# A four-level perceiver block on one Trainium2 core: first tile asked for first, the first MLP's norms interleaved between tiles, time mixing with its weights on ScalarE

## The chip, the cores and the metric

The kernel runs on one core of a Trainium2 chip. The metric is device time in microseconds (us) of one execution; three runs of the kernel before are given. One further execution was recorded by the hardware profiler. Engines are named as in the profile: PE is TensorE (PEld its weight loads), DVE is VectorE, ACT is ScalarE, POOL is GpSimd, SP is SyncE, which issues most transfers.

## The reference, cut to what matters

The input x has 8 sequences of 64 rows with 256 channels, 512 rows in all, in fp32; a context of 8 x 1601 x 128 stands beside it. Twelve blocks follow each other, each x = x + block(layernorm(x)): four levels of cross-attention over the context, self-attention or time mixing, and a mixture of experts. Two of them are touched. The first is level 0's cross-attention, which is a self-attention with an MLP, and then an attention over the context with an MLP:

```python
def _mha(x, y, ...):                                  # layernorm with gain and bias: _ln
    o = attention(_ln(x, lnx_g, lnx_b), _ln(y, lny_g, lny_b))
    x_out = x + o @ li1_w + li1_b
    h = gelu(_ln(x_out, ln3_g, ln3_b) @ li2_w + li2_b)
    return x_out + h @ li3_w + li3_b

x = _ln(xx, ln1_g, ln1_b)
x = x + _mha(x, x, a1...)          # self-attention, mask of future keys behind the softmax
x = _ln(x, ln2_g, ln2_b)
return x + _mha(x, ee, a2...)      # over the context
```

The second is level 1's time mixing, over k, v and r, three products of x mixed with its predecessor in the sequence:

```python
def step(carry, kv):               # one step in time, per channel
    aa, bb, pp = carry
    ww = u + kt;  p = maximum(pp, ww)
    y = (exp(pp - p) * aa + exp(ww - p) * vt) / (exp(pp - p) * bb + exp(ww - p))
    p2 = maximum(pp + w, kt);  e1b = exp(pp + w - p2);  e2b = exp(kt - p2)
    return (e1b * aa + e2b * vt, e1b * bb + e2b, p2), y
out = (sigmoid(r) * y) @ Wo        # w = -exp(time_decay), u = time_first
```

## The kernel before, in words

The 512 rows lie as NI = 4 tiles of P = 128 rows, `X[:, i, :]`, on the chip for the whole kernel. The outer order is the order of the blocks; inside a block the loops run over the four tiles, over the 16 heads and, for attention over the context, over 8 batches and 13 tiles of 128 context rows (KT). All transfers of weights, rows and the context are asked for on SP's queue, in program order, into rotating pools. Within an engine's queue, instructions run in order; what order they are put in is chosen by a scheduler from the program's text and dependencies, except where `manual_schedule(engines=...)` or `keep_in_program_order` fixes it. `FLASH` (L621) names PE, ACT and DVE for such regions.

A norm is `norm_of` (L343 to L347: statistics `bn_stats`, `bn_aggr`, eps added on DVE, then power -0.5 on GpSimd, 128x1) and `norm_by` (L351, subtract the mean and multiply, on DVE). `normed_tile` is both in one. Each norm so goes from DVE to GpSimd and back.

The start (L283 to L325, L1318 to L1326): x, `const` (identity, masks, rope tables), `cols` (per-channel gains and biases) and four weights are asked for, then three rows that are spread over all partitions: ln1_g, ln1_b, a1li1_b. `begin(i)` norms tile i, norms it again, multiplies by ln1_g, adds ln1_b, norms it a third time for the attention, and lets GpSimd make `xo` = x + a1li1_b. The transposes pst (L438), scaled on DVE (L446), feed the products psq and psk (L455), then the scores psS (L505).

The first MLP (L1395 to L1417): `norm1` and `enter1` run staggered over the tiles, with two base sums per tile on GpSimd (L1401, L1402); `turn_into` (L1279) transposes a tile on PE and scales its first chunk on ACT (L1289), its second on DVE (L1287). `after_attention` (L1299) is li2 with Gelu (psl, L396; L1303), then `meanwhile()`, then li3 (psn, L405), which calls `leave1(i)` for each tile: add base, norm, times ln2_g, plus ln2_b, norm again, and `turn2(i-2)`. Here `meanwhile` is `context_norm` (L1370): 12 GpSimd operations make `shift` for a later rope, statistics of the first context batch on DVE (L1355), four operations of `scales` on GpSimd (L1360 to L1363), 13 normalisings on ACT (L1368). Then follows a2wq (psl, 16 products) and the attention over the context.

The block m2 (L1489 to L1513) comes behind that attention: GpSimd makes x1r = x1 + a2li1_b and base = X + x1 + a2li3_b, four tiles each; the product of li1 gives psn, and `attended(i)` adds x1r, norms, and turns tile i-2 by `enter2`; GpSimd adds `xo` to base. Then the second MLP, whose last addition writes X.

Time mixing (L1677 to L1744) works channel-major: `xT` has 2 chunks (NC_) of 128 channels by 512 rows. Three mixings on DVE (L1694, L1695), three products on PE; kk and vv are copied out of PSUM, rr is a sigmoid on ACT (L1700). Per chunk: a scan for the running maximum pp (L1720), five differences on DVE with four exponentials on ACT for e1, e2, f1, f2 (L1721 to L1730), two scans for bb and aa (L1733, L1734), numerator and denominator, reciprocal (L1740), the product with rr, yy (L1743), and Wo (psn, L405).

## Time and profile before

| what | value |
|---|---|
| runs | 2094.94, 2100.58, 2097.62 us; median 2097.62 |
| profiled execution | 2095.15 us; its span 2093.4, 1.75 around it |
| granted PE clock, mean over the span | 0.947 |
| PE busy | 1885.6 us (90%) |
| DVE, ACT, POOL busy | 1246.5, 1031.0, 310.1 us |

The timeline gives start, duration, engine, line and operation, with out<-in by tile names; x16 means sixteen instructions in a row that were folded into one line, and the bracket holds the engine's idle time before it and what ended it. In the table of stretches, a busy time is followed by the number of instructions; PEclk is the clock that PE was granted, as a share of full speed. The places that the diff touches lie at 0 to 30 us (start), 83 to 133 us (first MLP), 585 to 605 us (m2) and 858 to 905 us (time mixing).

### The profile page before, as it was taken

Reading aid. Unit: us, or ns where it says so; the run is one execution under the profiler, and the core shown is the slowest. Engines: PE = TensorE matmul, PEld = TensorE weight load, DVE = VectorE, ACT = ScalarE, POOL = GpSimd, SP = SyncE. Lnnn points to the kernel's source line nnn. Section 1 sums busy time; section 2 is a strip of 40 time slices with the busy share of each in tenths; the row PEclk is TensorE's granted clock in tenths of the full one; section 3 lists DMA queues with packets and bytes.
Section 4 is the critical chain, followed back from the end, with each engine's and each line's share of the span. In section 5 each row is a group of like instructions: output and inputs, shape, how many; then the busy total and the mean of one; then the engine's idle time right before and its main releaser. Section 6 shows DMA issues by size and latency. Waiting matters only on the chain. (4 is left out here: it accounts for less than half of the span.)

```text
span 2093.4 us, 35785 instructions
## 1 busy us (share of the span) xinstructions
PE 1885.6 (90%) x14818; PEld 1363.0 (65%) x14818; DVE 1246.5 (60%) x2118; ACT 1031.0 (49%) x1703; POOL 310.1 (15%) x391
## 2 busy tenths in 40 slices
PE   5878999999989898659999999999967899998889
PEld 4545777777758475338757777778834566666747
DVE  5546666666716423660266666665634588888743
ACT  2326777777612222301166565654212788888323
POOL 3301111111033221030000000000023011211124
PEclk9989999999989898859999999999979999999989
DMA  8310000000005207215500010000422101000313
GB/s 299 113 56 1 18 17 17 18 17 11 1 30 213 86 28 268 103 43 197 181 17 33 33 33 33 33 17 16 177 78 82 39 18 34 18 18 16 137 56 112
DMA packets 37939, 142.16 MB, mean 68 GB/s; under 512 B 4904, under 2 KB 17712, under 8 KB 32208
## 3 DMA queue, kind: packets, MB, share of 16 engines
q1 hardware_dynamic: 32448, 128.18, 17.2%
q0 software_dynamic: 3696, 10.11, 1.4%
q8 instruction: 118, 1.93, 0.4%
q10 hardware_dynamic: 1632, 1.57, 0.2%
q14 instruction: 45, 0.37, 0.1%
HBM read 129.21 MB, written 19.71 MB: 71 GB/s over the span
## 5 line engine op out<-in xcount | busy, mean ns | idle before, releaser
L866 PEld LDWEIGHTS psav<-cn,raw 128*128 128x128 f32 (+1 forms) x3328 | 402.3, 191 | 87.1 <-issue 85.8
L801 DVE TENSOR_TENSOR raw<-raw,mb 128x1024 f32<-128x1024 f32 (+1 forms) x336 | 383.9, 1146 | 61.3 <-ACT mb L797 61.3
L866 PE MATMUL psav<-cn,raw 128*128 128x129 f32 (+1 forms) x3328 | 406.7, 275 | 0.7 <-ACT raw L805 0.7
L854 PE MATMUL psS<-qk,ct 128*128 128x512 f32 (+1 forms) x832 | 397.2, 599 | 7.5 <-ACT raw L855 7.5
L780 DVE TENSOR_TENSOR top<-raw,top 128x1024 f32<-128x1024 f32 (+1 forms) x240 | 271.4, 1131 | 143.1 <-ACT raw L855 121.8
L805 ACT ACTIVATE raw<-raw 128x1024 f32<-128x1024 f32 (+1 forms) x336 | 335.8, 1002 | 15.8 <-DVE raw L801 14.4
L855 ACT COPY raw<-psS 128x512 f32<-128x512 f32 (+1 forms) x416 | 236.6, 588 | 126.4 <-PE psS L854 123.2
L854 PEld LDWEIGHTS psS<-qk,ct 128*128 128x128 f32 (+1 forms) x832 | 138.1, 187 | 115.0 <-issue 81.5
L976 ACT COPY raw<-psS 128x1024 f32<-128x1024 f32 (+1 forms) x112 | 105.3, 940 | 2.0 <-PE psS L971 1.7
L774 DVE TENSOR_TENSOR top<-raw 128x1024 f32<-128x1024 f32 x48 | 58.8, 1225 | 71.1 <-ACT raw L855 37.7
L971 PEld LDWEIGHTS psS<-qz,kT 32*128 32x128 f32 (+1 forms) x1664 | 54.8, 181 | 61.2 <-ACT raw L976 42.2
L1215 PE MATMUL psgd<-w,xdT 128*128 x272 | 92.5, 472 | 1.5 <-DVE xdT L1204 1.5
L347 POOL TENSOR_TENSOR mv<-mv,mhalf 128x1 f32<-128x1 f32 x76 | 42.4, 562 | 339.5 <-DVE mv L346 319.0
L971 PE MATMUL psS<-qz,kT 32*128 32x128 f32 (+1 forms) x1664 | 76.9, 295 | 15.2 <-ACT raw L976 14.9
L992 PE MATMUL psav<-raw,v 128*32 128x128 f32 (+1 forms) x1664 | 86.3, 279 | 3.6 <-ACT raw L805 3.5
L992 PE MATMUL psav<-raw,ones 128*32 128x128 f32 (+1 forms) x1664 | 83.6, 273 | 0.0
L469 POOL MEMSET vz<- 128x528 f32 (+1 forms) x12 | 7.5, 644 | 427.6 <-PE pso L1853 427.4
L1241 POOL DMA_INDIRECT answered<-rows,homes x53 | 51.0, 963 | 95.7 <-ACT rows L1239 53.0
L1215 PEld LDWEIGHTS psgd<-w,xdT 128*128 128x128 f32 x272 | 48.6, 194 | 21.2 <-issue 9.0
L797 ACT COPY mb<-psmb 128x512 f32<-128x512 f32 x48 | 28.2, 588 | 67.3 <-PE psmb L795 67.1
L949 PE MATMUL psk<-ct,w_x3kv_None 128*128 128x401 f32 (+1 forms) x128 | 58.0, 539 | 0.7 <-issue 0.7
L959 PE MATMUL psv<-w_x3kv_None,ct 128*128 128x256 f32 (+1 forms) x208 | 55.6, 387 | 0.0
(429 smaller groups left out, 2829.4 us busy)
## 6 DMA issues: line engine op xcount, KB each, us to landing
cn<-in_cn_dram SPq DMA_DIRECT2D x24, 838.5 KB, 4.5
ct<-in_ct_dram SPq DMA_DIRECT2D x24, 800.5 KB, 4.5
dealt<-in_deal_dram SPq DMA_DIRECT2D x3, 2955.5 KB, 25.9
w<-in_f0w_dram SPq DMA_DIRECT2D x8, 1088.0 KB, 15.8
w_f1up<-in_f1up_dram SPq DMA_DIRECT2D x8, 1024.0 KB, 4.8
w_f1dn<-in_f1dn_dram SPq DMA_DIRECT2D x8, 1024.0 KB, 4.8
w<-in_f2w_dram SPq DMA_DIRECT2D x8, 1024.0 KB, 14.1
w<-in_f3w_dram SPq DMA_DIRECT2D x16, 384.0 KB, 7.8
```

The costliest lines, as they stand in the source:

```text
L774: nc.vector.tensor_tensor(hd["top"], hd["raw", 0], raw, ALU.max)
L780: nc.vector.tensor_tensor(top[:n, :m, :], raw, top[:n, :m, :], ALU.max)
L801: nc.vector.tensor_tensor(raw, raw, halves[h]["mb"][:n].unsqueeze(1).to_broadcast([n, m, 512]), ALU.add)
L805: nc.scalar.activation(raw, raw, AF.Exp)
L854: nc.tensor.matmul(x[:n], ct[:, kt * P : kt * P + n], qk, start=True, stop=True)
L855: nc.scalar.copy(raw[:n, i, :], x[:n])
L866: nc.tensor.matmul(oa[:, j // 2, j % 2 * CO : (j % 2 + 1) * CO], w[:n, i, j * P : (j + 1) * P], cn[:n, kt, :], start=kt == 0 and j % 2 == ...
L949: nc.tensor.matmul(t[:, : hi - lo], wkv[:, c * P : (c + 1) * P], cts[b][:, lo:hi], start=True, stop=True)
L971: nc.tensor.matmul(x[:n, g, i * P : (i + 1) * P], kTs[h][r, kt * P : kt * P + n], qzs[b][r, c].rearrange("p m s -> p (m s)"), start=True, ...
L976: nc.scalar.copy(raw[:n, :m, :].rearrange("p i (g s) -> p i g s", g=4), x[:n, :, : m * P].rearrange("p g (i s) -> p i g s", s=P))
L992: nc.tensor.matmul(oa[r, at * P : (at + 1) * P], what, w[:n, i, g * P : (g + 1) * P], start=kt == 0 and at == 0, stop=kt == KT - 1 and at ...
L1215: nc.tensor.matmul(y[:, :m], st[t]["xT"][:, k, :], w[:, bass.ds(x + at + k * m, m)], start=k == 0, stop=k == C // P - 1)
```

## The change

1. Start. Tile 0 of x is asked for alone and first; the rows ln1_g and ln1_b are asked for right behind it, on ACT's queue; `const` comes in two parts, the rope tables after the first weights, the rest of x after `cols`. In `begin`, the second norm's scaling and the two row operations become two `scalar_tensor_tensor`.
2. `turn_into` scales both chunks on ACT.
3. `context_norm` writes the two scaled tables to one temporary of two parts, and keeps its statistics in program order.
4. `leave1` uses the same two combined operations, and `norm_by` of tile i-1 (`scale2`) stands between the statistics and the use of tile i's; the MLP from li2 to the last `turn2` lies in a region of fixed order on PE, ACT, DVE and POOL (`FOUR`).
5. The sums xo = x1 + a2li1_b, X += x1, X += a2li3_b (12 on GpSimd) stand right behind the first MLP; m2 keeps X += xo only, with `norm_by` one tile late, and the second MLP adds straight into X.
6. Time mixing: k and r stay in PSUM; v is copied on ACT; the scaling in the mixing of v and r is on ACT; the pairs e1, e2 and f1, f2 are exp(-relu(d)) and exp(-relu(-d)) of one difference d, on ACT; sigmoid becomes a factor 1 + min(exp(-r), 1e36) in the denominator.

```diff
@@ -281,11 +281,16 @@
 X = keep.tile([P, NI, C], F32, tag="X", name="X")
-nc.sync.dma_start(X.rearrange("p i c -> p (i c)"), d["x"])
+nc.sync.dma_start(X[:, 0, :], d["x"][:, :C])
+first_rows = [rpool.tile([P, C], F32, tag="r", name="row") for _ in range(2)]
+for k, t in zip(("ln1_g", "ln1_b"), first_rows):
+    nc.scalar.dma_start(t, d["rows"][row_at[k] : row_at[k] + 1, :].partition_broadcast(P))
 const = keep.tile([P, d["const"].shape[1]], F32, tag="const", name="const")
-nc.sync.dma_start(const, d["const"])
+n0 = const_at["r0c"][0]
+nc.sync.dma_start(const[:, :n0], d["const"][:, :n0])
 cols = keep.tile([P, d["cols"].shape[1]], F32, tag="cols", name="cols")
 nc.sync.dma_start(cols, d["cols"])
+nc.sync.dma_start(X[:, 1:, :].rearrange("p i c -> p (i c)"), d["x"][:, C:])
@@ -619,6 +624,7 @@
+FOUR = FLASH | {mybir.EngineType.Pool}
@@ -1282,11 +1288,9 @@
     for c in range(C // P):
-        d = dst[:, c, i * P : (i + 1) * P]
-        if c:
-            nc.vector.tensor_scalar(d, t[:, c * P : (c + 1) * P], col(pair[0], c), col(pair[1], c), ALU.mult, ALU.add)
-        else:
-            nc.scalar.activation(d, t[:, c * P : (c + 1) * P], AF.Identity, bias=col(pair[1], c), scale=col(pair[0], c))
+        nc.scalar.activation(
+            dst[:, c, i * P : (i + 1) * P], t[:, c * P : (c + 1) * P], AF.Identity, bias=col(pair[1], c), scale=col(pair[0], c)
+        )
@@ -1310,7 +1314,8 @@
     li1 = chunks(weight("a1li1"), C)
-    g1, b1, r1 = row("ln1_g"), row("ln1_b"), row("a1li1_b")
+    nc.sync.dma_start(const[:, n0:], d["const"][:, n0:])
+    (g1, b1), r1 = first_rows, row("a1li1_b")
@@ -1318,9 +1323,9 @@
             normed_tile(y, X[:, i, :])
-            normed_tile(x, y)
-            nc.vector.tensor_tensor(x, x, g1, ALU.mult)
-            nc.vector.tensor_tensor(x, x, b1, ALU.add)
+            mv = norm_of(y)
+            nc.vector.scalar_tensor_tensor(x, y, mv[:, 0:1], g1, ALU.subtract, ALU.mult)
+            nc.vector.scalar_tensor_tensor(x, x, mv[:, 2:3], b1, ALU.mult, ALU.add)
@@ -1352,7 +1357,7 @@
-            nc.vector.bn_stats(st, cns[b][:, kt, :CY])
+            tc.keep_in_program_order(nc.vector.bn_stats(st, cns[b][:, kt, :CY]))
             nc.vector.bn_aggr(mvs[b][:, kt, 0:2], st)
@@ -1372,10 +1377,10 @@
                 cs, sn = (K(x)[:, c * P : (c + 1) * P] for x in ("r0c", "r0s"))
-                tmp = mp.tile([P, P], F32, tag="turned", name="turned", bufs=2)
-                nc.gpsimd.tensor_scalar(tmp, sn, col(k + "s", c), None, ALU.mult)
-                nc.gpsimd.tensor_scalar(dst, cs, col(k, c), None, ALU.mult)
-                nc.gpsimd.tensor_tensor(dst, dst, tmp, ALU.add)
+                tmp = mp.tile([P, 2, P], F32, tag="turned", name="turned", bufs=2)
+                nc.gpsimd.tensor_scalar(tmp[:, 0], sn, col(k + "s", c), None, ALU.mult)
+                nc.gpsimd.tensor_scalar(tmp[:, 1], cs, col(k, c), None, ALU.mult)
+                nc.gpsimd.tensor_tensor(dst, tmp[:, 0], tmp[:, 1], ALU.add)
 @@ -1389,8 +1394,8 @@
-        xn, z = (nat.tile([P, NI, C], F32, tag="nat", name="xn") for _ in range(2))
-        mvs1 = {}
+        xn = nat.tile([P, NI, C], F32, tag="nat", name="xn")
+        mvs1, mvs2 = {}, {}
@@ -1401,23 +1406,36 @@
         def leave1(i, t):
...
             nc.vector.tensor_tensor(x, t, base[:, i, :], ALU.add)
-            normed_tile(z[:, i, :], x)
-            nc.vector.tensor_tensor(x, z[:, i, :], g2, ALU.mult)
-            nc.vector.tensor_tensor(x, x, b2, ALU.add)
-            normed_tile(xn[:, i, :], x)
+            mv = norm_of(x)
+            scale2(i - 1)
+            nc.vector.scalar_tensor_tensor(x, x, mv[:, 0:1], g2, ALU.subtract, ALU.mult)
+            nc.vector.scalar_tensor_tensor(x, x, mv[:, 2:3], b2, ALU.mult, ALU.add)
+            mvs2[i] = norm_of(x)
             turn2(i - 2)
...
+        def scale2(i):
+            if i >= 0:
+                norm_by(xn[:, i, :], x1[:, i, :], mvs2[i])
...
         staggered(norm1, enter1)
-        after_attention("a1", xo, x3, mp, ps, leave1, context_norm)
-        turn2(NI - 2)
-        turn2(NI - 1)
+        with tc.manual_schedule(engines=FOUR):
+            after_attention("a1", xo, x3, mp, ps, leave1, context_norm)
+            turn2(NI - 2)
+            scale2(NI - 1)
+            turn2(NI - 1)
...
+        r1, r3 = row("a2li1_b"), row("a2li3_b")
+        for i in range(NI):
+            for dst, one, two in ((xo, x1[:, i, :], r1), (X, X[:, i, :], x1[:, i, :]), (X, X[:, i, :], r3)):
+                tc.keep_in_program_order(nc.gpsimd.tensor_tensor(dst[:, i, :], one, two, ALU.add))
     for dealt in dealts:
@@ -1487,31 +1505,30 @@
         with general() as ps, tc.tile_pool(name="m2", bufs=1) as mp:
-            r1, r3 = row("a2li1_b"), row("a2li3_b")
-            base, x1r = (mp.tile([P, NI, C], F32, tag=k, name=k) for k in ("base", "x1r"))
                 xn = nat.tile([P, NI, C], F32, tag="nat", name="xn")
-            for i in range(NI):
-                nc.gpsimd.tensor_tensor(x1r[:, i, :], x1[:, i, :], r1, ALU.add)
-            for i in range(NI):
-                nc.gpsimd.tensor_tensor(base[:, i, :], X[:, i, :], x1[:, i, :], ALU.add)
-                nc.gpsimd.tensor_tensor(base[:, i, :], base[:, i, :], r3, ALU.add)
+            mvs2 = {}
...
+            def scale2(i):
+                norm_by(xn[:, i, :], xo[:, i, :], mvs2[i])
+                nc.gpsimd.tensor_tensor(X[:, i, :], X[:, i, :], xo[:, i, :], ALU.add)
...
             def enter2(i):
                 turn_into(ps, x3, i, xn[:, i, :], ("a2ln3_g", "a2ln3_b"))
-                nc.gpsimd.tensor_tensor(base[:, i, :], base[:, i, :], xo[:, i, :], ALU.add)
...
             def attended(i, t):
-                nc.vector.tensor_tensor(xo[:, i, :], t, x1r[:, i, :], ALU.add)
-                normed_tile(xn[:, i, :], xo[:, i, :])
+                nc.vector.tensor_tensor(xo[:, i, :], t, xo[:, i, :], ALU.add)
+                mvs2[i] = norm_of(xo[:, i, :])
+                if i > 0:
+                    scale2(i - 1)
                 if i > 1:
...
             enter2(NI - 2)
+            scale2(NI - 1)
             enter2(NI - 1)
-            after_attention(
-                "a2", xo, x3, mp, ps, lambda i, t: nc.vector.tensor_tensor(X[:, i, :], t, base[:, i, :], ALU.add), lambda: None
-            )
+            after_attention("a2", xo, x3, mp, ps, into_X, lambda: None)
@@ -1687,61 +1704,75 @@
-    kk, vv, rr = big("kk"), big("vv"), big("rr")
-    for n, (k, w, dst) in enumerate((("k", wkv[:, 0:2], kk), ("v", wkv[:, 2:4], vv), ("r", wro[:, 0:2], rr))):
-        mixed = pool.tile([P, NC_, NT], F32, tag="mixed", name="mixed", bufs=2)
-        for c in range(NC_):
-            nc.vector.tensor_scalar(mixed[:, c, :], xT[:, c, :], col("time_mix_" + k, c), None, ALU.mult)
-            nc.vector.scalar_tensor_tensor(
-                b4(mixed)[:, c, :, 1:], b4(xT)[:, c, :, : S - 1], om[:, 2 * n + c : 2 * n + c + 1],
-                b4(mixed)[:, c, :, 1:], ALU.mult, ALU.add,
-            )
-        if k == "r":
-            lin_T(ps, w, mixed, C, lambda c, t: nc.scalar.activation(rr[:, c, :], t, AF.Sigmoid))
-        else:
-            lin_T(ps, w, mixed, C, lambda c, t: evac(dst[:, c, :], t))
...
+    at = lambda x, c: b4(x)[:, c]
+    old, new = (lambda x, c: at(x, c)[:, :, : S - 1]), (lambda x, c: at(x, c)[:, :, 1:])
+    first = lambda x, c: at(x, c)[:, :, 0:1]
+    head = lambda t: t.rearrange("p (b s) -> p b s", s=S)[:, :, 1:]
...
+    vv = big("vv")
+    kk, pr = {}, {}
+    leaves = (
+        lambda c, t: kk.update({c: t}), lambda c, t: nc.scalar.copy(vv[:, c, :], t), lambda c, t: pr.update({c: t}),
+    )
+    for n, (k, w) in enumerate((("k", wkv[:, 0:2]), ("v", wkv[:, 2:4]), ("r", wro[:, 0:2]))):
+        mixed = pool.tile([P, NC_, NT], F32, tag="mixed", name="mixed", bufs=2)
+        for c in range(NC_):
+            share = col("time_mix_" + k, c)
+            if n:
+                nc.scalar.activation(mixed[:, c, :], xT[:, c, :], AF.Copy, scale=share)
+            else:
+                nc.vector.tensor_scalar(mixed[:, c, :], xT[:, c, :], share, None, ALU.mult)
+            nc.vector.scalar_tensor_tensor(
+                new(mixed, c), old(xT, c), om[:, 2 * n + c : 2 * n + c + 1], new(mixed, c), ALU.mult, ALU.add,
+            )
+        lin_T(ps, w, mixed, C, leaves[n])
...
     decay, pp, e1, e2, ev = big("decay"), big("pp"), big("e1"), big("e2"), big("ev")
-    aa, bb, yy = big("aa"), big("bb"), big("yy")
+    f1, f2, de, df, er = big("f1"), big("f2"), big("de"), big("df"), big("er")
+    aa, bb, den = big("aa"), big("bb"), big("den")
     for c in range(NC_):
...
     nc.gpsimd.memset(g3(e1)[:, :, 0:1], 0.0)
-    at = lambda x, c: b4(x)[:, c]
-    old, new = (lambda x, c: at(x, c)[:, :, : S - 1]), (lambda x, c: at(x, c)[:, :, 1:])
-    pmax, f1, f2, den = big("pmax"), big("f1"), big("f2"), big("den")
+    nc.gpsimd.memset(g3(e2)[:, :, 0:1], 1.0)
+    nc.gpsimd.memset(g3(den)[:, :, 0:1], 1.0)
...
+    def weights(c, d, one, two):
...
+        for x, sign in ((one, 1.0), (two, -1.0)):
+            nc.scalar.activation(new(x, c), new(d, c), AF.Relu, scale=sign)
+            nc.scalar.activation(new(x, c), new(x, c), AF.Exp, scale=-1.0)
...
     for c in range(NC_):
-        nc.vector.tensor_tensor_scan(pp[:, c, :], decay[:, c, :], kk[:, c, :], 0.0, ALU.add, ALU.max)
-        nc.vector.scalar_tensor_tensor(new(e1, c), old(pp, c), wd[:, c : c + 1], new(pp, c), ALU.add, ALU.subtract)
-        nc.scalar.activation(new(e1, c), new(e1, c), AF.Exp)
-        nc.vector.tensor_tensor(e2[:, c, :], kk[:, c, :], pp[:, c, :], ALU.subtract)
-        nc.scalar.activation(e2[:, c, :], e2[:, c, :], AF.Exp)
-        u = col("time_first", c)
-        nc.vector.scalar_tensor_tensor(new(pmax, c), new(kk, c), u, old(pp, c), ALU.add, ALU.max)
-        nc.vector.tensor_tensor(new(f1, c), old(pp, c), new(pmax, c), ALU.subtract)
-        nc.scalar.activation(new(f1, c), new(f1, c), AF.Exp)
-        nc.vector.scalar_tensor_tensor(new(f2, c), new(kk, c), u, new(pmax, c), ALU.add, ALU.subtract)
-        nc.scalar.activation(new(f2, c), new(f2, c), AF.Exp)
+        nc.vector.tensor_tensor_scan(pp[:, c, :], decay[:, c, :], kk[c], 0.0, ALU.add, ALU.max)
+        nc.vector.scalar_tensor_tensor(new(de, c), head(kk[c]), wd[:, c : c + 1], old(pp, c), ALU.subtract, ALU.subtract)
+        weights(c, de, e1, e2)
+        nc.vector.scalar_tensor_tensor(new(df, c), head(kk[c]), col("time_first", c), old(pp, c), ALU.add, ALU.subtract)
+        weights(c, df, f1, f2)
+        nc.scalar.activation(er[:, c, :], pr[c], AF.Exp, scale=-1.0)
...
+        nc.vector.tensor_scalar(er[:, c, :], er[:, c, :], 1.0e36, 1.0, ALU.min, ALU.add)
     for c in range(NC_):
+        nc.vector.tensor_tensor_scan(bb[:, c, :], e1[:, c, :], e2[:, c, :], 0.0, ALU.mult, ALU.add)
         nc.vector.tensor_tensor(ev[:, c, :], e2[:, c, :], vv[:, c, :], ALU.mult)
-        nc.vector.tensor_tensor_scan(bb[:, c, :], e1[:, c, :], e2[:, c, :], 0.0, ALU.mult, ALU.add)
         nc.vector.tensor_tensor_scan(aa[:, c, :], e1[:, c, :], ev[:, c, :], 0.0, ALU.mult, ALU.add)
...
         nc.vector.tensor_tensor(new(den, c), new(den, c), new(f2, c), ALU.add)
+        nc.vector.tensor_tensor(den[:, c, :], den[:, c, :], er[:, c, :], ALU.mult)
         nc.vector.tensor_tensor(new(f2, c), new(f2, c), new(vv, c), ALU.mult)
...
         nc.vector.tensor_tensor(new(f1, c), new(f1, c), new(f2, c), ALU.add)
-        nc.vector.reciprocal(new(den, c), new(den, c))
-        nc.vector.tensor_tensor(new(f1, c), new(f1, c), new(den, c), ALU.mult)
-        nc.scalar.copy(at(f1, c)[:, :, 0:1], at(vv, c)[:, :, 0:1])
-        nc.vector.tensor_tensor(yy[:, c, :], f1[:, c, :], rr[:, c, :], ALU.mult)
-    lin_nat(ps, wro[:, 2:4], yy, into_X)
+        nc.scalar.copy(first(f1, c), first(vv, c))
+        nc.vector.reciprocal(den[:, c, :], den[:, c, :])
+        nc.vector.tensor_tensor(f1[:, c, :], f1[:, c, :], den[:, c, :], ALU.mult)
+    lin_nat(ps, wro[:, 2:4], f1, into_X)
```

## The prediction

> **What bounds the kernel now.** The page comes first. TensorE is busy for nine tenths of the span, so only the places where it isn't can give time.
>
> ```profile
> PE 1885.6 (90%) x14818; PEld 1363.0 (65%) x14818; DVE 1246.5 (60%) x2118; ACT 1031.0 (49%) x1703; POOL 310.1 (15%) x391
> ```
>
> The diff touches four such places, and they are read in the timeline of core 0 (start, duration, engine, line, operation; in brackets the idle time before it and what ended it). The start:
>
> ```profile
> 4.20 0.43 DVE L343 BATCH_NORM_STATS2 st<-X 128x6 f32<-128x256 f32 x1 [4.20 <-DMA X<-in_x_dram]
> ...
> 13.37 0.43 DVE L1322 TENSOR_TENSOR x<-x,row_ln_g 128x256 f32<-128x256 f32 x1 [3.50 <-DMA row_ln_g<-in_rows_dram]
> ...
> 14.33 0.73 POOL L1326 TENSOR_TENSOR xo<-x,row_a1li_b 128x256 f32<-128x256 f32 x1 [4.91 <-DVE x L1323]
> ...
> 16.44 0.69 PE L438 MATMUL pst<-const,xn 128*128 128x128 f32 x2 [16.44 <-DVE xn L351]
> ```
>
> DVE waits 4.20 us for x and 3.50 us more for row ln1_g. The way out of the first MLP:
>
> ```profile
> 110.32 0.42 DVE L1406 TENSOR_TENSOR x<-psn,base 128x256 f32<-128x256 f32 x1 [16.62 <-PE psn L405]
> ...
> 115.50 0.42 DVE L1406 TENSOR_TENSOR x<-psn,base 128x256 f32<-128x256 f32 x1
> ...
> 130.53 0.41 DVE L351 TENSOR_SCALAR xn<-x,mv 128x256 f32<-128x256 f32 x1 [0.39 <-POOL mv L347]
> ...
> 132.68 9.18 PE L396 MATMUL psl<-T,w_a2wq_None 128*128 128x512 f32 x16 [1.00 <-DVE T L1287]
> ```
>
> DVE takes four tiles from 110.32 to 130.94, some 5 us each, with two waits for GpSimd's power in each; PE has nothing else to do until 132.68. The same before the second MLP (m2):
>
> ```profile
> 590.48 0.15 DVE L346 TENSOR_SCALAR mv<-mv 128x1 f32<-128x1 f32 x1
> ...
> 595.27 0.58 POOL L347 TENSOR_TENSOR mv<-mv,mhalf 128x1 f32<-128x1 f32 x1
> ...
> 595.89 0.64 DVE L351 TENSOR_SCALAR xn<-xo,mv 128x256 f32<-128x256 f32 x1 [5.26 <-POOL mv L347]
> ...
> 605.38 16.92 PE L396 MATMUL psl<-T,w_a2li_None 128*128 128x512 f32 x32 [0.55 <-ACT T L1289]
> ```
>
> The power asked for at 590.63 stands behind GpSimd's sums and runs at 595.27. Time mixing, in the timeline and the table of stretches (length, then PE, PEld, DVE, ACT, POOL, clock, DMA share, GB/s):
>
> ```profile
> 904.24 3.78 PE L405 MATMUL psn<-w_r1b_None,yy 128*128 128x256 f32 x8 [3.92 <-DVE yy L1743]
> ```
>
> ```profile
> 880.00:896.00 16.00, 0.00 (x0) 0.00 (x0) 16.00 (x20) 4.84 (x8) 0.00 (x0) 0.64 0.00 0
> ```
>
> Here DVE is the bound without a gap, and GpSimd does nothing at all.
>
> **Start.** X (512 KB) was asked for at 0.74 and there at 4.20. A quarter of it I put at 3.2, an estimate: the stretch from 0 to 30 moved 355 GB/s, so 384 KB less are some 1.05 us. Rows g and b are asked for at once, so the 3.50 us goes; so do the 2.38 us in which DVE waited at 9.45 for a power that stood behind four shift operations (6.51, 2.36 us; in the changed order they stand behind, with the other shift operations). A norm of 0.41 and two products of 0.43 become two combined operations of about 0.43 (-0.4). From 4.20 to 16.44 were 12.24; 12.24-3.50-1.6 (of the 2.38, the power itself and its way take 0.8)-0.4 = 6.7, so the first transpose starts at about 9.9: 6.5 us. Not all of it arrives. Row a1li1_b, for GpSimd's first sum xo, keeps its place on SP's queue, issued near 6.2 behind 3.7 MB (512+818+34+4x512+2x128 KB), and took 7.8 us to land: there at 13.9 as before, when xo (0.73) was last to need it. So xo now ends at 14.7. GpSimd is in order: behind it stands the power of tile 1's second norm (0.55), for that DVE's whole queue waits, the scaling of qz with it. DVE resumes at 15.24 where it did at 19.64, 4.4 earlier, and the scores psS start at 21.6 against 25.17, 3.5 earlier. The two issues on ACT's queue stand ahead of nothing but the table load, since ACT's first work is at 21.26; SP issues one transfer more ahead of wq (0.45), and wq and wk, there by about 8, still bind nothing. From there on each tile follows the one before, so I carry it to the end at 3.7; bounds 0 (rows late as before) to 6.5 (r1 in time).
> The Trainium skill (DMA: Bandwidth & Descriptors, "Issuing engines are not separate DMA queues") says that transfers of all issuing engines interleave on the same 16 engines, so that a second queue saves the issue alone; if g and b so landed no earlier than 13.37, the start would give nothing and the total below would be 13.5 in place of 17.2. No row here shows two queues at once.
>
> **First MLP.** The front (83 to 90) stays: the power of tile 3 still stands behind the base sums (87.17). Both chunks of a transposed tile go through ACT: 0.46 each, pitch 0.39, against DVE's 0.41 after ACT's: 0. The shifts' 12 GpSimd operations (8 at 0.60, 4 at 0.45, 6.6 us) all run after 89.1 now, none at 6.51; then the scales (0.28+2.48+0.22+0.29, 3.3): GpSimd is free at 99, the first power is due at 111.69. ACT does 8 Gelus before 13 normalisings (0.42 each, 107.6 to 113.1); the first evacuation behind them is due at 117.4. Both hidden.
> A tile on DVE: sum 0.46, statistics 0.46, 0.21 and 0.20, previous tile's norm in the power's shade (0.57, in all 0.85), two combined operations at 0.52, statistics 0.89: 3.9. From 110.32: four tiles to 125.9, a power 0.65 and a norm: 127.0 to 127.2 against 130.94. PE delivers a tile each 3.6 at 117 to 121, just below. Gain 3.9; bounds 2.5 (cadence 4.2) and 4.4 (PE's pace 3.75).
>
> **GpSimd's sums.** 12 at 0.72 are 8.7 us, now at 127 to 136, under psl (9.18) where DVE waits 5.84 and 2.74 for PE: 0. If they disturb: the norm that ran beside such a sum took 0.81 (87.75) against 0.41, so tile 3's could lose 0.4. The Trainium skill (GPSIMD Engine Reference, "Key points") has GpSimd share SBUF interfaces with VectorE and contend when an instruction has two SBUF inputs; applied to all that DVE does in these 9 us at the row's factor of two, and nothing hidden, it would take the whole 3.9 back and make the total 13.3. The waits of 5.84 and 2.74 speak for 0.
>
> **m2.** With x1r and base gone, the power runs at 590.7 and the norm at 591.3, 4.6 earlier. PE is through with the 24 products of three tiles at 593.5, then transposes tile 0 and makes tile 3's product; DVE goes on with some 2.3 us a tile (0.46+0.46+0.21+0.20, norm in the power's shade, 0.41 and waits), as before at 596.45 to 601.18. Its last norm ends near 599.0 against 604.09, and psl starts at 600.25 against 605.38. Of the 20 sums (14.4 us) 4 stay, X+=xo, behind each power: the next power may wait 0.3, inside the bounds. Gain 5.1; bounds 3.5 (a transpose missed and made a tile later) and 5.5.
>
> **Time mixing.** DVE loses four scalings (0.42 each, 1.6), the copies of kk and vv (1.2), three of five differences per chunk (3.74) and yy (1.2); it gains er (0.84) and den*er (1.2): 5.7 net. But its queue now waits for ACT: 16 Relu/Exp of 0.55 follow each other, and after the first chunk's scan (871.2) and the r mixing (876.1) it stands until e2 is there at about 878.3, 0.85 idle. Reading kk from PSUM may cost 0.4. Walked through: first reciprocal 884.6 to 887.8 (it was at 889.16), then the second chunk's two scans (1.13 each), five 0.60 us products and sums and den*er, second reciprocal 895.25 to 898.45, last product to 899.7 against 904.2. Two table loads (1.28 each) go from ACT. Gain 4.5; bounds 1.0 (ACT's pairs a full chunk behind, 3.5 more idle) and 5.7.
>
> **Sum.** 3.7+3.9+5.1+4.5 = 17.2. The profiled execution took 2095.15 (span 2093.4 and 1.75 around it): 2078.0. The runs' median 2097.62 stands 2.47 higher, so 2080.4 there. The least that measurement can tell is 0.3%, 6.3 us.
>
> **PE's clock** may add. It falls to 0.50 some 3 us into a pause, and psl then starts at half speed: 9.18 for 16 products that take 0.43 each warm (6.9), 16.92 for 32 (13.7): 2.3 and 3.2 lost. I leave both in; were the shorter pauses to keep it warm, 5.5 more.
>
> **Rivals.**
> - More: r1 in time, all at the upper bounds (22.1), clock warm (5.5): 2070.0 in the median's terms. For: pauses shorten by 4 and 5 us. Against: lone transposes did not hold the clock before. 0.12.
> - Part: all at the lower bounds, 0+2.5+3.5+1.0 = 7.0: 2090.6. For: ACT carries 16 more operations in mixing. 0.12.
> - No change: the start gives nothing and GpSimd is late by about 10 at 111.7, 17.2-3.7-10 = 3.5 left: 2094. 0.08.
> - Slower: in the fixed order every power of the MLP's way out stands behind shifts and scales. These 9.9 us have from 89.1 to 111.7. GpSimd's scale operations (L1360) took 1.09 to 1.17 beside attention's DVE work against 0.28 here, a factor of 4. At 4 all of it lasts 39.6 us, to 128.7: 17.0 late. With 3.9 kept and the others low (0+3.5+1.0), 8.6 slower: 2106.2. It is late from a factor of 2.3 and decides from 3.8. Against: DVE does only statistics then, beside which the power took 2.48. 0.05.
> - Forecast: 0.63. Faster is 0.63+0.12+0.12 less 0.03 that the part case loses to measurement, 0.84; same 0.10; slower 0.06. The range runs from 2070 to the part case.
>
> **What would show it.** Right: PE's first transpose near 10 and psS near 21.6, with GpSimd's first xo ended by r1; tiles of the MLP's way out each 3.9 and psl 7.6 earlier than 132.68, near 125.1 (start included); the first norm of m2 0.7 after its request; DVE from 864.64 to its last operation in 35 in place of 39.6, without sigmoid's table loads. Wrong: first xo not waiting; GpSimd not free at the first power; psl after the pauses at 0.43 each; DVE idle over 2 us in mixing, or time lost in attention (150 to 560), where nothing is touched.

## The result and the profile after

The changed kernel took 2077.57 us (median of 4 runs, 2076.49 to 2077.98) against 2097.32 for the kernel before (4 runs, 2094.94 to 2100.58): a ratio of 0.9906, interval 0.9893 to 0.9918. It is faster by 19.75 us where 17.2 were forecast, and inside the range. The profiled execution took 2076.49, its span 2074.7, so 18.70 were won between the two spans. The sums below are made on that number.

On the page, PE's share hardly moves; DVE lost 10 us and 30 instructions:

```profile
PE 1886.7 (91%) x14818; PEld 1366.1 (66%) x14818; DVE 1236.6 (60%) x2088; ACT 1038.5 (50%) x1725; POOL 311.3 (15%) x393
```

Where the 18.70 came from is read from mark to mark in the two timelines. The granted clock, mean over the span, is 0.951 against 0.947.

| stretch (from mark to mark) | before | after | won | forecast |
|---|---|---|---|---|
| start to the first sum of `leave1` | 110.32 | 105.49 | 4.83 | 3.7 |
| that sum to psl of a2wq | 22.36 | 16.97 | 5.39 | 3.9 |
| psl of a2wq to the next product | 10.17 | 11.12 | -0.95 | 0 |
| attention over the context | 440.48 | 440.37 | 0.11 | 0 |
| m2: last products of a2wv (pso), li1, to psl of the second MLP | 22.05 | 15.87 | 6.18 | 5.1 |
| that psl to its psn | 16.76 | 15.27 | 1.49 | 0 |
| second MLP's end, L0 self-attention, level 1's first attention | 229.99 | 234.78 | -4.79 | 0 |
| time mixing, to Wo's psn | 48.46 | 42.42 | 6.04 | 4.5 |
| the rest | 1189.16 | 1188.75 | 0.41 | 0 |

The four parts won 22.4, 5.2 more than forecast. The other five rows took 3.7 of it back on balance; the largest loss, 4.79, stands in a stretch of 230 us that the diff doesn't touch (called "the stretch" below).

The start, in the timeline of after:

```profile
5.34 0.43 DVE L348 BATCH_NORM_STATS2 st<-X 128x6 f32<-128x256 f32 x1 [5.34 <-DMA X<-in_x_dram]
...
8.13 0.47 DVE L1327 SCALAR_TENSOR_TENSOR x<-t,mv,row 128x256 f32<-128x256 f32 x1
...
11.73 0.69 PE L443 MATMUL pst<-const,xn 128*128 128x128 f32 x2 [11.73 <-DVE xn L356]
...
14.99 0.73 POOL L1331 TENSOR_TENSOR xo<-x,row_a1li_b 128x256 f32<-128x256 f32 x1 [3.25 <-DMA row_a1li_b<-in_rows_dram]
```

DVE waits for no row at 8.13, but it waits for tile 0 until 5.34, later than for the whole x before (4.20). The first transpose comes 4.7 earlier. Then GpSimd's xo waits 3.25 us for row a1li1_b, which lands at 14.99, and the scores start at 21.53.

The way out of the first MLP:

```profile
105.49 0.42 DVE L1412 TENSOR_TENSOR x<-psn,base 128x256 f32<-128x256 f32 x1 [16.41 <-PE psn L410]
...
108.94 0.42 DVE L1412 TENSOR_TENSOR x<-psn,base 128x256 f32<-128x256 f32 x1
...
116.07 0.42 DVE L1412 TENSOR_TENSOR x<-psn,base 128x256 f32<-128x256 f32 x1 [0.21 <-PE psn L410]
...
120.19 0.72 POOL L1438 TENSOR_TENSOR xo<-x,row_a2li_b 128x256 f32<-128x256 f32 x1
...
120.26 0.80 DVE L356 TENSOR_SCALAR xn<-x,mv 128x256 f32<-128x256 f32 x1 [0.73 <-POOL mv L352]
...
122.46 10.13 PE L401 MATMUL psl<-T,w_a2wq_None 128*128 128x512 f32 x16 [0.90 <-ACT T L1291]
```

The tiles follow at 3.45, 3.45 and 3.68 us. In the trace DVE has no gap of 0.2 us from the second sum to the last, which waits 0.21 for PE's psn: DVE has caught up with PE. The first tile (0.46) and the last norm (0.73) alone wait for a power. That last norm runs beside the first of the moved sums and takes 0.80 instead of 0.41. The psl behind takes 10.13 against 9.18.

In m2 the first power now comes 0.08 us after its request's end, and the norm 0.70 after that request:

```profile
580.67 0.15 DVE L351 TENSOR_SCALAR mv<-mv 128x1 f32<-128x1 f32 x1
...
580.90 0.58 POOL L352 TENSOR_TENSOR mv<-mv,mhalf 128x1 f32<-128x1 f32 x1
...
581.52 0.41 DVE L356 TENSOR_SCALAR xn<-xo,mv 128x256 f32<-128x256 f32 x1 [0.70 <-POOL mv L352]
...
589.82 15.43 PE L401 MATMUL psl<-T,w_a2li_None 128*128 128x512 f32 x32 [0.55 <-ACT T L1291]
```

In time mixing DVE waits 1.98 us for k's product and 0.69 for ACT, and no more:

```profile
851.93 0.88 DVE L1729 TENSOR_SCALAR mixed<-T,cols 128x512 f32<-128x512 f32 x2
...
857.41 1.22 DVE L1754 TENSOR_TENSOR_SCAN pp<-decay,psl 128x512 f32<-128x512 f32 x1 [1.98 <-PE psl L401]
...
864.53 1.23 DVE L1763 TENSOR_TENSOR_SCAN bb<-e,e 128x512 f32<-128x512 f32 x1 [0.69 <-ACT e L1751]
...
870.68 3.35 DVE L1773 RECIPROCAL den<-den 128x512 f32<-128x512 f32 x1
...
885.95 3.78 PE L410 MATMUL psn<-w_r1b_None,f 128*128 128x256 f32 x8 [5.44 <-DVE f L1774]
```

Its queue runs from 851.93 to 885.89, 33.96 us in place of 39.6. The same places before:

```profile
864.64 0.88 DVE L1694 TENSOR_SCALAR mixed<-T,cols 128x512 f32<-128x512 f32 x2
...
871.31 0.69 DVE L336 COPY kk<-psl 128x512 f32<-128x512 f32 x1 [2.26 <-PE psl L396]
...
889.16 3.31 DVE L1740 RECIPROCAL den<-den 128x504 f32<-128x504 f32 x1
```

**The stretch.** Its loss is read with a measure: PE's busy time in each 1-us slice, times 2(1 - granted clock), summed. That is the time that PE worked at half clock; about half of it is lost. In the stretch this is 22.0 us before and 33.4 after, so 11.4 more, some 5.7 us lost, which covers the 4.79. It begins in L0's self-attention, with the second tile's scores:

```profile
635.28 2.04 PE L510 MATMUL psS<-qkr,qz 64*128 64x64 f32 x32 [1.36 <-ACT qz L619]
...
641.14 1.91 PE L460 MATMUL psw<-xT,w_b0q_None 128*128 128x128 f32 x8
```

Before, the same place of the same tile reads:

```profile
652.33 2.00 PE L505 MATMUL psS<-qkr,qz 64*128 64x64 f32 x32 [1.35 <-ACT qz L614]
...
656.32 1.06 PE L455 MATMUL psw<-xT,w_b0q_None 128*128 128x128 f32 x8
```

The pause is 1.35 or 1.36 us in both, and the scores take the same 2.0. Yet eight products behind them take 1.91 in place of 1.06. The table of stretches (columns as in the prediction) gives the clock around them, first after, then before:

```profile
639.00:641.00 2.00, 2.00 (x11) 2.00 (x11) 0.84 (x1) 1.06 (x1) 0.00 (x0) 0.50 1.01 422
```

```profile
656.00:658.00 2.00, 2.00 (x21) 2.00 (x20) 0.85 (x1) 1.06 (x1) 0.00 (x0) 1.00 1.02 427
```

Same work on DVE and ACT, same transfers, half the clock and half the products.

### The profile page after: what moved, and what is told of

It reads as the page before. It is cut to its first block, busy times and chain, and to the rows that moved or that the text cites. A ratio compares the mean times of both kernels' runs of the same rounds, so it can differ in the third digit from the quotient of the medians.

```text
span 2074.7 us, 35787 instructions
## 1 busy us (share of the span) xinstructions
PE 1886.7 (91%) x14818; PEld 1366.1 (66%) x14818; DVE 1236.6 (60%) x2088; ACT 1038.5 (50%) x1725; POOL 311.3 (15%) x393
## 5 line engine op out<-in xcount | busy, mean ns | idle before, releaser
L811 ACT ACTIVATE raw<-raw 128x1024 f32<-128x1024 f32 (+1 forms) x336 | 335.4, 1001 | 15.8 <-DVE raw L807 14.4
L860 PEld LDWEIGHTS psS<-qk,ct 128*128 128x128 f32 (+1 forms) x832 | 138.3, 187 | 114.9 <-issue 81.6
L998 PE MATMUL psav<-raw,ones 128*32 128x128 f32 (+1 forms) x1664 | 83.5, 273 | 0.0
```

The lines of the kernel that those rows point to most:

```text
L811: nc.scalar.activation(raw, raw, AF.Exp)
L860: nc.tensor.matmul(x[:n], ct[:, kt * P : kt * P + n], qk, start=True, stop=True)
L998: nc.tensor.matmul(oa[r, at * P : (at + 1) * P], what, w[:n, i, g * P : (g + 1) * P], start=kt == 0 and at == 0, stop=kt == KT - 1 and at ...
```

## The experiments

Theory: the four parts give what their stages show, each by the mechanism of the prediction (row waits gone, norms interleaved, GpSimd's queue cleared, DVE's work cut), and none pays for another; the difference from 17.2 is in their sizes. Rivals: the gains are shifts, and what one part wins is waited off later ("residue"); the sums' new place costs what their old one did; and the loss in the stretch comes from one of the parts and not from the clock. A ratio is to the kernel before, run on the same chip. Profiled executions are compared with 2095.15 (before) or 2076.49 (after).

### The start: its two halves, and the row a1li1_b

**e1_start_only**: on before, the start alone (x, rows and `const` in their new order, the two combined operations); `shift` is made as before.

```diff
-nc.sync.dma_start(X.rearrange("p i c -> p (i c)"), d["x"])
+nc.sync.dma_start(X[:, 0, :], d["x"][:, :C])
+for k, t in zip(("ln1_g", "ln1_b"), first_rows): nc.scalar.dma_start(t, ...)
-            normed_tile(x, y)
+            mv = norm_of(y)   # and two scalar_tensor_tensor
```

> Before, with the start alone changed (tile 0 and rows first, const in two parts, combined operations in begin); the shifts are written as before. In this kernel's order of instructions GpSimd has the first shift operation behind the first two powers, and it reads the second part of const, which landed near 14.6 in the changed kernel. Theory (the start pays only because the shifts move away): tile 0's third power waits for that part, PE's first transpose comes at 15.5 to 17 (before 16.44, changed kernel 11.73), no gain in the start, -1 to +1 us in all. Rival (the start's gain is its own): first transpose at 11.7, scores psS at 21.5, 4.4 us less. In the untouched stretch from the first statistics behind the second MLP (626.25 before) to the first psn of the next level's attention (855.78), 229.5 before and 234.3 in the changed kernel: the theory of the clock (only PE's granted clock differs there) allows anything from 229 to 235, in step with time at half clock; the rival that the change itself leaves something behind there expects 229.5.

Measured: 2094.73, ratio 0.9995 (0.9986 to 1.0004): nothing that can be told. The timeline shows why:

```profile
14.67 0.61 POOL L1383 TENSOR_SCALAR shift<-const,cols 128x128 f32<-128x128 f32 x1 [5.53 <-DMA const<-in_const_dram]
15.27 0.56 POOL L352 TENSOR_TENSOR mv<-mv,mhalf 128x1 f32<-128x1 f32 x1
...
16.38 0.69 PE L443 MATMUL pst<-const,xn 128*128 128x128 f32 x2 [16.38 <-DVE xn L356]
```

A `shift` operation stands on GpSimd ahead of a power and waits for the rope tables, which the change asks for later. Its 5.53 us take the whole gain.

**e2_start_shift**: e1 and part 3 of the change, the `shift` operations with a temporary of two parts.

```diff
-                tmp = mp.tile([P, P], F32, tag="turned", name="turned", bufs=2)
+                tmp = mp.tile([P, 2, P], F32, tag="turned", name="turned", bufs=2)
```

> As the run before, and the shifts are made as in the changed kernel, so that GpSimd has them behind the base sums of the first MLP. Both theories of the start: first transpose at 11.7, the first sum xo waits for row a1li1_b until 15.0, psS at 21.5, the maximum mx near 24.9 (before 29.26); 4.4 us earlier at the first sum behind the first MLP (105.9 for 110.32). In all 4.4 less by this part, 2090.8 on the profiled execution's scale, plus or minus what the clock does in untouched places (theory: up to 5 us either way; rival: 0).

Measured: 2090.84, ratio 0.9973 (0.9964 to 0.9982); first transpose 11.98, scores 21.54, the first sum of `leave1` 4.29 earlier. So the start pays only because part 3 lets the scheduler place `shift` behind the powers.

**e6_r1_early**: after, with a1li1_b as the third row on ACT's queue.

```diff
-    for k, t in zip(("ln1_g", "ln1_b"), first_rows):
+    for k, t in zip(("ln1_g", "ln1_b", "a1li1_b"), first_rows):
         nc.scalar.dma_start(t, d["rows"][...].partition_broadcast(P))
```

> The changed kernel, with row a1li1_b asked for on ACT's queue too, as the third row, in place of SP's queue behind the weights. Theory (the prediction's step: the first sum xo stands on this row and holds GpSimd and by it DVE): xo runs when x is there (about 9.6), the power of tile 1's second norm at 14.25 in place of 15.68, the second combined operation at 14.9 in place of 16.26, psS 0.8 to 1.4 us earlier than 21.53. X of tile 0 lands 0 to 0.5 later than 5.34 for 128 KB more at its side. In all 0.5 to 1.4 us less than the changed kernel. Rival (the row binds nothing: qz and vz follow other work): psS at 21.5 all the same.

Measured: 2077.53, ratio 0.9904 (0.9888 to 0.9919), the same as after. xo waits for no row now, and tile 0 lands at 5.59:

```profile
5.59 0.43 DVE L348 BATCH_NORM_STATS2 st<-X 128x6 f32<-128x256 f32 x1 [5.59 <-DMA X<-in_x_dram]
...
9.87 0.73 POOL L1331 TENSOR_TENSOR xo<-x,row 128x256 f32<-128x256 f32 x1 [0.60 <-DVE x L1328]
```

The scores start at 20.56, 0.97 earlier; time mixing ends 2.0 ahead of after. Behind it 3.0 are lost again (1191.8 against 1188.8), with 80.3 us at half clock (the measure of the stretch above) against 73.7. m2, with the same text as in after, took 16.61 in place of 15.87: its first sum comes 6.02 behind the products of a2wv in place of 5.58, with PE's psn of 24 products at 8.18 in place of 7.02.

**e7_rows_sp**: the three rows on SP's queue, behind x's tile 0, `const`'s first part and `cols`.

```diff
 nc.sync.dma_start(cols, d["cols"])
+for k, t in zip(("ln1_g", "ln1_b", "a1li1_b"), first_rows):
+    nc.sync.dma_start(t, d["rows"][...].partition_broadcast(P))
```

> The changed kernel, with the three rows asked for on SP's queue, right behind tile 0 of x, the first part of const and cols, and nothing on ACT's queue. Theory (tile 0 landed at 5.34, later than all of x before, because two rows moved beside it on the same engines): tile 0 is there at 3.4 to 4.4, the rows by 7, the first transpose 1 us earlier than 11.73, no wait of xo, psS 1 to 2 us earlier than 21.53. Rival (a small transfer in rows of 1 KB is no faster than 4.6 us from issue): tile 0 at 5.3 as before, first transpose at 11.7 or later if the rows bind.

Measured: 2075.01, ratio 0.989 (0.9874 to 0.9905).

```profile
3.11 0.43 DVE L348 BATCH_NORM_STATS2 st<-X 128x6 f32<-128x256 f32 x1 [3.11 <-DMA X<-in_x_dram]
...
10.61 0.69 PE L443 MATMUL pst<-const,xn 128*128 128x128 f32 x2 [10.61 <-DVE xn L356]
```

Tile 0 lands 2.23 us earlier than in after, so the two rows beside it on ACT's queue cost it that; the scores start at 20.23. The stretch took 230.2, its half clock 21.8. Here too the part behind mixing is longer (1192.8, at 75.7 us of half clock against 73.7). Of the 4.0, 2.7 stand at its front. From Wo's psn to the last copy of the next context attention's query product (qT), e7 takes 141.65 in place of 138.91, with 30.7 us at half clock in place of 25.1; the sum over the whole part hides this, since e7 has less half clock at the end. Over all kernels this front takes 138.8 to 139.2 us with 24.8 to 25.8 at half clock, and in e6, e7, e9, e10 and e11 141.5 to 141.7 with 30.6 to 32.7. With intervals that overlap, e7 isn't shown to beat after.

### The first MLP

**e3_mlp1_only**: on before, parts 2 to 4 of the change (both chunks on ACT, `shift`, `leave1` with `scale2`, the fixed order); the sums stay in m2.

```diff
+            scale2(i - 1)
+            nc.vector.scalar_tensor_tensor(x, x, mv[:, 0:1], g2, ALU.subtract, ALU.mult)
-            after_attention("a1", xo, x3, mp, ps, leave1, context_norm)
+            with tc.manual_schedule(engines=FOUR):
+                after_attention("a1", xo, x3, mp, ps, leave1, context_norm)
```

> Before, with the first MLP's way out alone changed (both chunks on ACT, shifts, statistics in order, combined operations, norm one tile late, fixed order on four engines); the sums for the second MLP stay where they were. Theory: a tile costs DVE 3.45 to 3.7 where it cost 5, psl of a2wq starts 5.4 us before its old 132.68, near 127.3; the start is as before to 0.5 us. No norm runs beside a sum, so the last norm takes 0.41 and not 0.80, 0.4 more. Rival (fixed order makes GpSimd late): powers wait behind shifts, gain under 2. In all 5 us less, plus or minus the clock.

Measured: 2091.97, ratio 0.9979 (0.997 to 0.9988). The way out took 16.57 in place of 22.36, and psl starts 5.59 earlier, at 127.09. Of this, 2.5 are gone again by the end of the attention over the context (443.0 against 440.5, half clock 9.8 us against 5.8), and 2.1 in the stretch (232.1, half clock 26.2). So the stage pays in full, and 4.6 of its 5.59 are given back where half clock has grown; with what other stages gain (0.71 in m2), the median lies 4.4 below that of before.

**e8_free_order**: after, without the region of fixed order.

```diff
-            with tc.manual_schedule(engines=FOUR):
-                after_attention("a1", xo, x3, mp, ps, leave1, context_norm)
+            after_attention("a1", xo, x3, mp, ps, leave1, context_norm)
```

> The changed kernel without the region of fixed order in the first MLP: the scheduler then puts the norm of each of the first three tiles ahead of the next tile's sum and statistics on DVE, mixes ACT's normalisings with the Gelus, and leaves GpSimd's order all but alone. Theory (half of the MLP's gain is the shade that each power finds): each of three tiles waits for its power again, 0.6 to 0.9 each, psl of a2wq 1.8 to 2.7 us later than 122.46. Rival (PE's products set the pace, a tile each 3.45): at most 0.5 later.

Measured: 2081.53, ratio 0.9923 (0.991 to 0.9937). The norms wait for their powers again:

```profile
111.16 0.41 DVE L356 TENSOR_SCALAR xn<-x,mv 128x256 f32<-128x256 f32 x1 [0.67 <-POOL mv L352]
115.62 0.41 DVE L356 TENSOR_SCALAR xn<-x,mv 128x256 f32<-128x256 f32 x1 [0.66 <-POOL mv L352]
```

A tile takes 4.5 us, the way out 20.12 against 16.97. That is 3.15 for the fixed order, more than the 1.8 to 2.7 that I expected; psl comes 4.66 later in all, the other 1.5 being there already at the first sum, ahead of anything that the edit names. The scores start at 21.53 in both; between them and the first MLP, e8 has 10.7 us of half clock and after 8.1.

### GpSimd's sums and time mixing

**e4_sums_only**: on before, part 5 alone.

```diff
+            for i in range(NI):
+                for dst, one, two in ((xo, x1[:, i, :], r1), (X, X[:, i, :], x1[:, i, :]), (X, X[:, i, :], r3)):
+                    tc.keep_in_program_order(nc.gpsimd.tensor_tensor(dst[:, i, :], one, two, ALU.add))
-                for i in range(NI):
-                    nc.gpsimd.tensor_tensor(x1r[:, i, :], x1[:, i, :], r1, ALU.add)
```

> Before, with the GpSimd sums behind the first MLP and the block m2 alone changed. Theory: the first norm of m2 follows its request by 0.8 in place of 5.3; psl of the second MLP starts 6.2 us earlier than 605.38, near 599.2, if nothing changes ahead of it; the 12 sums run under psl of a2wq and cost the attention nothing (the first norm beside a sum 0.8 in place of 0.41 at most). Rival (the sums take the time back behind the first MLP): psl of a2wq or the first scores come 1 to 4 us later than 132.68 and 147.76. Rival of the residue: the stretch 626.25 to 855.78 takes 234.3 in this kernel too, since it alone of the four has the changed end of the second MLP; the theory of the clock ties it to half-clock time.

Measured: 2089.39, ratio 0.9967 (0.9955 to 0.9979). m2 took 16.68 in place of 22.05: 5.37, less than expected. Of this, 0.40 stands ahead of m2's first sum (5.61 behind the products of a2wv in place of 6.01), where the psn of 24 products took 7.05 in place of 8.07. In their new place the 12 sums cost the last norm beside them 0.4 (0.81 in place of 0.41): the way out took 22.75 in place of 22.36. The psl behind it then ran 0.39 faster, so the next product starts at 142.54, in before at 142.85. The attention in between took 1.9 longer, with its half clock at 174 to 181 us instead of 164 to 171 and hardly more of it (6.1 us against 5.6); that the place makes the difference isn't shown. The stretch took 229.9: nothing waited off there.

**e9_mix_only**: on before, part 6 alone.

```diff
-        nc.vector.tensor_tensor(e2[:, c, :], kk[:, c, :], pp[:, c, :], ALU.subtract)
-        nc.scalar.activation(e2[:, c, :], e2[:, c, :], AF.Exp)
+            nc.scalar.activation(new(x, c), new(d, c), AF.Relu, scale=sign)
+            nc.scalar.activation(new(x, c), new(x, c), AF.Exp, scale=-1.0)
```

> Before, with time mixing alone changed. Theory: all of its gain stands in its own stage, as in the changed kernel: from the first psn of the attention ahead of it to the last psn of time mixing 42.4 in place of 48.5, 6 us; the last product's DVE chain without two table loads. In all 6.0 less than before, 2089 on the profiled execution's scale, plus or minus the clock elsewhere (nothing ahead of 855 is changed, so the stretch ahead should take its old 229 to 230). Rival (part of the 6 us is a clock that came with the other parts' shift in time): 4.5, as predicted.

Measured: 2092.34, ratio 0.9975 (0.9965 to 0.9984). The stage took 42.71 in place of 48.46 (5.75 won); the stretch ahead of it stayed at 230.0. Behind it 3.1 went again (1192.25 against 1189.16; half clock 81.6 us against 74.7). The execution shows 2.78. The first mixing comes 8.89 behind the last psn ahead of the stage, as in before (8.86); in after it is 8.40, with that psn at 1.99 in place of 2.58 (e9: 2.62).

The medians of e2, e3, e4 and e9 lie 5.5, 4.4, 7.0 and 4.1 us below those of before on their chips: 21.0 together, against 19.75 for the whole change. Nothing in this says that one part pays for another; each of the four has an interval of some 2 us to both sides.

### The clock in the stretch

**e5_warm_attn**: after, with products that nobody reads in L0's self-attention: three ahead of each tile's scores, two ahead of the first half of the transposes of pr.

```diff
+            if bv == "b0v":
+                keep_warm(x, 3)     # nc.tensor.matmul(t[:, :512], ident, const[:, :512], ...)
...
+                if bv == "b0v" and not g:
+                    keep_warm(t, 2)
```

> The changed kernel, with matrix products that nobody reads in level 0's self-attention only: per tile three (128x512) ahead of the scores psS and two ahead of the transposes psp, where PE waits for ACT; they are extra work, 20 x 0.43 us. Theory (the 4.8 us given back between the second MLP and level 1 are PE at half clock after pauses): the clock stays full in this attention, psq and psw of the third tile take 1.1 and not 1.9 to 2.0, and the stretch from the second MLP's first sum to the first psn of level 1's attention takes 229 to 231 in place of 234.8; 3 to 5 us faster than the changed kernel, 2073. Rival (something else than the clock, so that extra products only cost): the stretch stays at 234.8 or grows by up to 8.6.

Measured: 2085.63, ratio 0.9946 (0.9932 to 0.9959): worse than after. The clock was 1.00 from 612 to 686 us, but the stretch took 243.2, 8.4 more. Each product took 0.86 us, where I had reckoned with 0.43 (a product of 512 columns in fp32 is two instructions of 0.43). Three of them outlast the pause of 1.36.

**e10_warm_attn_small**: after, with one such product ahead of each tile's scores.

```diff
+            if bv == "b0v":
+                keep_warm(x, 512)
```

> The changed kernel, with one product (128x512) that nobody reads ahead of each tile's scores in level 0's self-attention, 4 in all, 0.86 us each, where PE waited 1.3 us for ACT; in place of the earlier 20, which kept the clock full there but outlasted the pauses. Theory of the clock: half-clock time of PE in this attention falls from 10.1 us to under 4, and the stretch from the second MLP's first sum to level 1's attention's first psn takes 230 to 232.5 in place of 234.8; 2.5 to 4.8 us faster than the changed kernel. Rival (the clock is not what lengthens it): 234.8 or up to 3.4 more. In between, if one product is too little to hold the clock: half-clock time stays near 10 and the stretch at 234.8 to 236.

Measured: 2074.74, ratio 0.9896 (0.9881 to 0.9911). Half clock in L0's self-attention fell from 10.1 us to 0.0, and the stretch from 234.78 to 231.99. The products that took 1.91 take 1.06 again:

```profile
632.25 1.02 PE L465 MATMUL psS<-const 128*128 128x512 f32 x2
...
638.62 1.06 PE L460 MATMUL psw<-xT,w_b0q_None 128*128 128x128 f32 x8
```

So the loss in the stretch is the clock's: with the clock held and nothing else changed, 2.8 of the 4.79 us come back, though 0.86 a tile is added to PE's work. That the whole kernel is faster than after isn't shown, the intervals overlap; the part behind mixing took 2.3 more.

**e11_warm_gaps**: e7, with such products in the two pauses that the change shortened, the way out of the first MLP and m2.

```diff
+            WARM1 = ((), (), (512,), (512, 512, 512))
-                    turn_into(ps, xT2, i, xn[:, i, :], ("a2lnx_g", "a2lnx_b"))
+                    turn_into(ps, xT2, i, xn[:, i, :], ("a2lnx_g", "a2lnx_b"), WARM1[i])
...
+                keep_warm(ps.tile([P, 512], F32, tag="ps", name="psw"), 256)
```

> The kernel with the three rows on SP's queue, and products that nobody reads in the pauses of the two places that wait for norms: between the last transposes of the first MLP's way out (one, three, and a half one) and of the second MLP's way in (one, two, and a half one). Theory of the clock: psl of a2wq takes 6.9 to 7.5 us in all for its 16 in place of 10.1, psl of the second MLP 13.7 to 14.2 for its 32 in place of 15.4; 3 to 5 us faster than the same kernel without them (2075.0), 2070 to 2072, if the clock elsewhere stays as it is. Rival (the pauses are too short for the extra products, and they end late): the start of each psl 0.5 to 2 later and nothing gained.

Measured: 2069.92, ratio 0.9877 (0.986 to 0.9893). psl of a2wq took 7.13 for its 16 in place of 9.80 in e7, that of the second MLP 14.00 in place of 17.06, both as the theory says. The interval overlaps with that of e7 and touches that of after, so the gain in all isn't shown by this run alone.

**e12_warm_all**: e11 and e10's product together.

```diff
+            if bv == "b0v":
+                keep_warm(x, 512)
```

> The run before, with one product ahead of each tile's scores in level 0's self-attention too. Theory: where the clock is full there anyway, 0 to 0.5 us are lost (the kernel with rows on SP's queue had 0.1 us of half clock there); where the shift in time of the run before has brought half clock back, 2.5 to 4.8 are won by it. 2070 to 2072.5. Rival: as the run before plus 3.4 us.

Measured: 2069.01 (4 runs, 2067.71 to 2069.95), ratio 0.9868 (0.9853 to 0.9884). Its interval lies below that of after: it beats both kernels. Both psl run at 0.44 to 0.45 a product:

```profile
119.09 7.13 PE L401 MATMUL psl<-T,w_a2wq_None 128*128 128x512 f32 x16 [0.46 <-ACT T L1299]
...
587.44 14.00 PE L401 MATMUL psl<-T,w_a2li_None 128*128 128x512 f32 x32
```

These are 3.0 and 1.4 us less than in after. m2 took 16.65, 0.8 more than in after, with its psn of 24 products at 8.46 in place of 7.02. L0's half clock is 0 again, but the attention over the context took 443.6 (half clock 10.1 us, in after 5.8): the clock was lost at another place. Against e11 the interval overlaps, so e10's product isn't shown to add to the pauses'.

Over all kernels the stretch follows its half clock, whatever was changed elsewhere:

| kernel | stretch | at half clock |
|---|---|---|
| before, e1, e2, e4, e9 | 229.9 to 230.1 | 21.6 to 22.0 |
| e7 | 230.2 | 21.8 |
| e3 | 232.1 | 26.2 |
| after, e8 | 234.8, 234.6 | 33.4 |
| e6 | 235.3 | 32.3 |
| e10, e12 | 232.0 | 22.7, 22.8 |
| e11 | 232.1 | 25.5 |

(e5 is left out, its products outlast the pauses; in e10 and e12 they add 0.86 a tile.)

## Why the prediction was right, point by point

- **Where the time is.** Right: all four stages gave, by the mechanisms named, and each gave more than its term, three of them more than the upper bound that I had set (4.4, 5.5 and 5.7). That the total came out near is partly luck, two misses that cancel: 5.2 more from the parts, 3.7 back elsewhere, for which the sum had nothing. Of the 22.4, 0.9 is PE's clock inside two of the stages (0.43 in m2, 0.46 in time mixing).
- **Start, 3.7; measured 4.83.** Of the steps, "a quarter of it I put at 3.2" failed: tile 0 landed at 5.34, because two rows ran beside it (e7, with the rows behind it on SP's queue: 3.11). "Rows g and b are asked for at once, so the 3.50 goes" held: DVE took the row at 8.13 without a wait. The first transpose came at 11.73, not 9.9. That r1 ends last was right, at 14.99 where I said 13.9: SP's queue stood until 5.82 with the issue of wv, 2.1 us that the profile puts down to the first of the two rows on ACT's queue. The scores then began at 21.53, as forecast (21.6), but by two misses that cancel: DVE resumed at 16.26 where I had 15.24, and from there to the scores it took 5.27 where I had 6.4 (5.53 before). The remaining 1.2 can't be called a gain of the change: between the scores and the first sum of `leave1` the kernels with the text of after up to there took 84.0 (after), 83.5 (e10), 85.5 (e5) and 85.5 (e8), those with the text of before 85.2 (before), 83.6 (e4) and 83.7 (e9). What I took as a minor step, the `shift` operations "stand behind", is what the whole start hangs on (e1 against e2).
- **The skill's rule on the start.** The Trainium skill (DMA: Bandwidth & Descriptors, "Issuing engines are not separate DMA queues") says that transfers from all engines share the 16 DMA engines and interleave. For tile 0 it held, 5.34 beside ACT's rows against 3.11 on one queue; what I had drawn from it for the rows themselves, that they would land no earlier than 13.37, did not.
- **First MLP, 3.9; measured 5.39.** The terms of the tile, added up as they stand, make 4.1; they make 3.9 if the 0.20 for eps is taken as part of the 0.85, as in the row (111.45 to 112.30). The mis-sized term is the tile, 3.45 instead of 3.9, and in it "previous tile's norm in the power's shade (0.57, in all 0.85)". In the trace of after the second tile's eps ends the statistics at 110.08, the previous norm starts at 110.15 and the first combined operation already at 110.47: it uses the mean alone and needs no power. The power is wanted by the second one, at 111.06, and is there. So a tile's first power costs DVE 0.39 in place of 0.85. Another 0.34 came behind the last norm, 1.40 to psl in place of 1.74, with its transposes at 0.44 in place of 0.69. e8 shows what the fixed order holds of the stage, 3.15. GpSimd was not late by the forecast's measure: the tiles between waited for no power.
- **GpSimd's sums, 0.** Right but for the 0.4 that I allowed for the last norm: 0.80 in place of 0.41. The way out shows it both ways, 22.75 with the sums in e4 against 22.36 without, 16.97 in after against 16.57 in e3. A loss of the whole 3.9, as if all of DVE's work slowed down beside the sums, did not come.
- **m2, 5.1; measured 6.18.** The norm 0.7 after its request was right. The sums alone give 5.37 (e4), of which 0.40 is PE's clock ahead of the first sum, so 5.0; both chunks of `turn_into` on ACT give 0.7 more (m2 21.34 in e3), a gain that I had put at 0. In after, too, 0.43 of the 6.18 stands ahead of the first sum and goes with the clock (e6, with the same text in m2, does not have it). My 20 sums of 14.4 us were misread: the trace has 16, 11.5 us, of which 4 stay.
- **Time mixing, 4.5; measured 6.04.** The waits for ACT were right: from the first scan to the scan for bb DVE took 7.12 (857.41 to 864.53, 0.69 of it idle), where my walk has 7.1 (871.2 to 878.3). The mis-sized term is the start of the first scan. I put it at 871.2, 6.56 behind the first mixing, as if k's product came as before; it started 5.48 behind it, 1.08 earlier. In before DVE's copy of k follows the sixth of PE's instructions (866.23 to 871.31), in after the scan follows the fourth (853.52 to 857.41). So the first reciprocal began 18.75 after the first mixing (870.68 against 851.93), where it was 24.52 before and my walk has 19.96. Reading kk from PSUM, for which I allowed 0.4, cost the scan nothing (1.22 against 1.23). DVE's queue took 33.96, where I said 35. Another 0.46 stands ahead of it, between the last psn and the first mixing, and goes with PE's clock: e9, without it, gains 5.75.
- **PE's clock.** I left it in, for the two psl. It fell there much as forecast: psl of a2wq lost 0.95 more, the second won 1.49. That it falls "some 3 us into a pause" is too simple for the trace of before: at 123.2 it fell 2.0 us into a pause (from 121.21), and at 597.7 PE had paused for 3.05 and was at work again since 596.58. The place where it cost most, L0's self-attention, was not in the text at all; of the signs that I gave for being wrong, "time lost in attention" is the one that came, in another attention than the one I named.
- **Rivals.** "More" needed r1 in time and a warm clock; neither came by itself, and e12, which gives both, took 2069.01 where that rival said 2070.0, though with 3.1 lost in the attention over the context, which its sum doesn't have. "Slower" asked for GpSimd 17 us late in the fixed order: the first power there kept DVE waiting 0.46.
